# The order of work inside a tick of a fused convolution and wavelet kernel: the channel mix between two Toeplitz products, the group sums and signs at the tick's begin

## The chip, the cores and the metric

The kernel runs on one core of a Trainium2 chip. The metric is device time in microseconds (us); lower is better. Before the change three runs took 2979.06, 2980.12 and 2980.6 us, so the median is 2980.12 us. One further execution was profiled, and all rows of the profile come from it.

Engines are called as the profile calls them: PE is the matrix engine and PEld its weight loads, DVE is VectorE, ACT is ScalarE, SP is the queue that issues nearly all DMAs.

## The reference, cut to what matters

Four layers act on x, which has 4 batches, 64 channels and 256 by 256 pixels, all in float32. Layers 0, 1 and 3 are long convolutions. Their kernels are outer products of a row filter and a column filter, so each is two products with Toeplitz matrices, one along each axis, plus x times a bias per channel. Layer 2 goes to Haar coefficients, scales them, mixes the 64 channels, thresholds, and goes back:

```python
f1 = haar2d(x)
acc = jnp.zeros_like(f1[:, :conv_w.shape[1]])
for i in range(v.shape[0]):                              # 2
    f3 = f1 * v[i]
    f4 = jnp.einsum('bchw,oc->bohw', f3, conv_w[i])
    f5 = jnp.sign(f4) * jax.nn.relu(jnp.abs(f4) - tau[i])
    acc = acc + f5
y = haar2d(acc, inverse=True)
return y + x
```

Since v does not depend on the channel, the kernel applies it after the mix: "products with v" below are scalings of the mixed coefficients.

## The kernel before, in words

**Units.** The convolution stages work on one channel of one batch at a time. A channel goes through five stages, one tick apart: its loads; the first product of layer 0 (PSUM tile pa, copied by ACT at line 199 to the SBUF tile a0); the second product of layer 0 (PSUM tile py, read by DVE at line 212 to y0); the first product of layer 1 (pa again, copied to a1); the second product of layer 1 (py, read to y1) with the sums and differences of pairs (lines 257 and 258). Below, a0, y0, a1 and y1 name these tiles, and pa0, py0, pa1 and py1 their products on PE. Each product is four matmul calls (lines 190 and 191), eight instructions. Further stages follow a channel later: Haar levels on four channels at a time (lines 269 and 270), a split into two parts (ACT line 280, DVE line 281), a product pz (line 288), its copy (ACT line 296) and its store (line 297).

The mixing stage works on groups of four coefficient rows of one batch, 64 groups a batch. `mix` multiplies with the channel weights (PSUM tile px, line 340) and scales with v: four of sixteen columns by one DVE instruction (line 357), twelve by one ACT instruction each (line 359); for the last batch ten and six. `shrink` takes the magnitude and the sign on ACT (lines 365 and 366) and subtracts tau on DVE (line 367). `signed` multiplies both (line 372), and `add` sums the two terms into z (line 376). These four stages of a group are also one tick apart.

**Stages of the run.** First the convolutions of batch 0 alone. Then, for each batch b, the mixing of b runs together with the convolutions of batch b+1, and after it the inverse of b (lines 390 to 440) with what is left of them. In the mixing of batch 0 the 64 channels of batch 1 are spread over 82 ticks; in those of batches 1 and 2 the channels of the next batch are spread over 72 ticks, so that about one tick in nine starts no channel. With the last batch's mixing run 63 convolutions of layer 3 that were put off.

**Order.** Nothing is issued at once. Every stage of every unit is put on a list as (tick, place, number), and the list, sorted, gives the program order (line 497). Within a tick a lower place comes first. The convolution stages have the places 0 (loads), -1 (pa0), -2 (py0), -3 (pa1), -4 (py1). A scheduler then takes instructions of each engine by that priority as it believes their inputs and buffers to be ready, and adds the waits; what it makes of the list is fixed when the program is built, and each engine and DMA queue then works strictly through its own list. Tiles rotate through buffers: four PSUM buffers for pa, py and pz, two for px, two SBUF buffers for a0 and a1 together, five for the Toeplitz tiles, three for y0, two each for the tiles of magnitudes and of signs.

Of the kernel before, what the change touches and what calls it, by code (L numbers as in the profile page):

```python
# [37 lines left out]
def conv_seq_kernel(ctx, tc, x, fz, fw, bias, decay, haar, haar_row, factors, vt, taut, wmix, out):  # L38
# [189 lines left out]
    def at(tick, place, run, unit):  # L228
        events.append((tick, place, len(events), run, unit))
# [86 lines left out]
    def mixing(b, start, n_act):  # L316

        st = {}

        def load(g):  # L320
            f = mx.tile([P, 2, S], F32, name=f"f_{b}_{g}", tag="f", bufs=3)
            nc.sync.dma_start(f, coef[b].rearrange("k c p w -> (k c) p w")[:, 2 * g : 2 * g + 2])
            st[g] = {"f": f}
            if g % GT == 0:
                t = mx.tile([P, 2, GT, 16], F32, name=f"vt_{b}_{g}", tag="vt")
                nc.sync.dma_start(t, scales[g // GT])
                st["vt", g // GT] = t

        def scale(g, i):
            return st["vt", g // GT][:, i, g % GT, :]  # L330

        def over(g, i, n):
            return scale(g, i)[:, :n].unsqueeze(2).to_broadcast([P, n, C])

        def mix(g):
            f = st[g]["f"]
            ps = psx.tile([P, 2, 2, S], F32, name=f"px_{b}_{g}", tag="mix")
            for q in range(2):
                for h in range(2):
                    nc.tensor.matmul(  # L340
                        ps[:, h, q, :],
                        f[:, q, h * P : (h + 1) * P],
                        wb.rearrange("p r n -> p (r n)"),
                        start=True,
                        stop=True,
                    )
            if g == 0:

                one, two = ps[:, :, 0, :P], ps[:, :, 0, P:]
                d = mx.tile([P, 2, P], F32, name=f"d_{b}", tag="mag")  # L350
                nc.vector.tensor_copy(d, two)
                nc.vector.tensor_sub(two, one, d)
                nc.vector.tensor_add(one, one, d)
            f4 = mx.tile([P, 16, C], F32, name=f"f4_{b}_{g}", tag="f4")
            px = ps.rearrange("p h q (r i o) -> p (h q r i) o", r=2, i=2)
            n = 16 - n_act
            nc.vector.tensor_tensor(f4[:, :n], px[:, :n], over(g, 0, n), ALU.mult)  # L357
            for j in range(n, 16):
                nc.scalar.mul(f4[:, j], px[:, j], scale(g, 0)[:, j : j + 1])  # L359
            st[g]["f4"] = f4  # L360

        def shrink(g):
            f4 = st[g]["f4"]
            mag = mx.tile([P, 16, C], F32, name=f"mag_{b}_{g}", tag="mag")
            nc.scalar.activation(mag, f4, AF.Abs)  # L365
            nc.scalar.activation(f4, f4, AF.Sign)  # L366
            nc.vector.tensor_sub(mag, mag, over(g, 1, 16))  # L367
            st[g]["mag"] = mag

        def signed(g):  # L370
            mag = st[g]["mag"]
            nc.vector.scalar_tensor_tensor(mag, mag, 0.0, st[g]["f4"], ALU.max, ALU.mult)  # L372

        def add(g):
            parts = st.pop(g)["mag"].rearrange("p (h r i) o -> p h r i o", h=2, i=2)
            nc.vector.tensor_add(z[:, :, 4 * g : 4 * g + 4, :], parts[:, :, :, 0, :], parts[:, :, :, 1, :])  # L376

        for g in range(S // 4):
            at(start + g - 2, 0, load, g)
            for s, stage in enumerate([mix, shrink, signed, add]):  # L380
                at(start + g + s, -1 - s, stage, g)

    def inverse(b, start, put_off):

# [98 lines left out]
    start = ready + 3  # L483
    for b in range(B):
        mixing(b, start, 12 if b + 1 < B else 6)
        end = start + groups + 3
        if b + 1 < B:
            ready = convolutions(b + 1, spread(ahead, end + 2), in_parts=range(C), border=end)
        else:
            convolution(  # L490
                [(i, c) for i in range(B - 1) for c in sorted(put_off)], spread(start - 2, end + 2, (B - 1) * len(put_off))
            )
        inverse(b, end, put_off if b + 1 < B else ())

        start = max(end + C, ready + 3)
        ahead = start - 3
# [111 lines left out]
```

## Time and profile before

| | |
|---|---|
| median of three runs | 2980.12 us |
| profiled execution | 2980.9 us, of which span 2979.1 us |
| PE busy | 2919.6 us (98%) |
| DVE busy | 2546.2 us (85%) |
| ACT busy | 2168.8 us (73%) |
| DMA | 218 GB/s on average |
| mixing of batches 0, 1, 2, 3, first to last product with v | 459 to 862, 1096 to 1534, 1772 to 2211, 2445 to 2719 us |

A busy PE is not PE at its peak: matmuls overlap each other, and their ends are modelled, so that a short stop is partly hidden in the durations. The idle time of an engine is put down to the last thing it waited for. The three figures of a wait are the sum in us, the number of times, and the longest.

### The profile page before, as it was taken

The page shows a single profiled execution, that of the slowest core. Times are in us where ns is not written, and L with a number is a line of the kernel's source. Part 1 is how long each engine was busy: PE and PEld are TensorE (multiplying, and loading weights), DVE is VectorE, ACT ScalarE, POOL GpSimd, SP SyncE. Part 2 cuts the span into 40 slices and gives each one's busy share as a digit, 9 for nine tenths or more (in the row PEclk, how much of TensorE's full clock was granted, in tenths as well). Part 3 has the DMA queues.
Part 4 walks back from the last instruction along what each step waited for, and adds up shares of the span by engine and source line. Part 5 has one row for each costly group of instructions (what it writes and reads, how often), then busy time and mean ns, then how long its engine had stood idle before and what let it go on. Part 6 is the DMA issues. An engine that isn't in the chain of part 4 may idle for free. (4 is left out here: it accounts for less than half of the span.)

```text
span 2979.1 us, 51970 instructions
## 1 busy us (share of the span) xinstructions
PE 2919.6 (98%) x16950; PEld 2614.5 (88%) x16950; DVE 2546.2 (85%) x4571; ACT 2168.8 (73%) x5014; POOL 0.2 (0%) x4
## 2 busy tenths in 40 slices
PE   8999999999999999999999999999999999999999
PEld 6899988888888988888888988888888988888998
DVE  4767768999998879999989878999988889998776
ACT  2333338999986668999986758999986768887554
POOL 0000000000000000000000000000000000000000
PEclk9999999999999999999999999999999999999999
DMA  5877776666667876666667876666767877777766
GB/s 157 253 232 227 231 228 215 204 208 198 204 204 245 249 216 204 208 211 204 210 211 244 254 218 197 208 214 204 207 214 236 255 232 233 233 230 219 211 212 186
DMA packets 562497, 649.73 MB, mean 218 GB/s; under 512 B 44369, under 2 KB 447412, under 8 KB 562100
## 3 DMA queue, kind: packets, MB, share of 16 engines
q1 hardware_dynamic: 482996, 562.07, 63.6%
q10 hardware_dynamic: 79232, 84.34, 8.0%
q8 instruction: 137, 2.24, 0.3%
q14 instruction: 132, 1.08, 0.1%
HBM read 426.77 MB, written 219.48 MB: 217 GB/s over the span
## 5 line engine op out<-in xcount | busy, mean ns | idle before, releaser
L190 PE MATMUL py<-t,a 128*128 128x256 f32 x3072 | 928.4, 384 | 30.5 <-ACT a L199 26.1
L199 ACT COPY a<-pa 128x512 f32<-128x512 f32 x768 | 477.1, 623 | 411.6 <-PE pa L191 382.0
L359 ACT ACTIVATE f<-px,vt 128x64 f32<-128x64 f32 x2688 | 582.9, 353 | 108.5 <-DVE f L357 108.2
L191 PEld LDWEIGHTS py<-t,a 128*128 128x128 f32 x3072 | 583.3, 190 | 79.4
L191 PE MATMUL py<-t,a 128*128 128x128 f32 x3072 | 590.0, 274 | 0.0
L190 PEld LDWEIGHTS py<-t,a 128*128 128x128 f32 x3072 | 487.3, 191 | 85.6 <-ACT a L199 52.6
L340 PE MATMUL px<-wb,f 128*128 128x256 f32 x2048 | 496.5, 380 | 4.3 <-ACT f L359 4.3
L340 PEld LDWEIGHTS px<-wb,f 128*128 128x128 f32 x2048 | 365.0, 191 | 43.6 <-ACT f L359 6.8
L367 DVE TENSOR_TENSOR mag<-mag,vt 128x1024 f32<-128x1024 f32 x256 | 312.7, 1222 | 22.5 <-ACT mag L365 18.7
L403 ACT CAST w<-pw 128x512 fp32r<-128x512 f32 x256 | 150.4, 587 | 225.1 <-PE pw L401 218.9
L372 DVE SCALAR_TENSOR_TENSOR mag<-mag,f 128x1024 f32<-128x1024 f32 x256 | 312.0, 1219 | 1.1
L190 PE MATMUL pa<-t,y 128*128 128x256 f32 x1024 | 306.5, 381 | 2.0 <-DVE y L212 2.0
L190 PE MATMUL pa<-t,x 128*128 128x256 f32 x1024 | 305.5, 380 | 0.9 <-issue 0.9
L365 ACT ACTIVATE mag<-f 128x1024 f32<-128x1024 f32 x256 | 292.0, 1141 | 9.4 <-DVE z L376 6.8
L393 ACT COPY zc<-z 128x512 f32<-128x512 f32 x256 | 281.8, 1102 | 2.0 <-ACT w L403 1.2
L366 ACT ACTIVATE f<-f 128x1024 f32<-128x1024 f32 x256 | 275.3, 1075 | 5.8 <-DVE y L212 0.7
L281 DVE TENSOR_TENSOR sp<-sd,sp 128x512 fp32r<-128x512 f32 x256 | 176.3, 689 | 102.1 <-ACT sp L280 99.2
L190 PE MATMUL pa<-t,u 128*128 128x256 f32 x772 | 232.7, 383 | 3.2 <-PE pu L413 1.9
L212 DVE SCALAR_TENSOR_TENSOR y<-x,bsb,py 128x512 f32<-128x512 f32 x256 | 190.4, 744 | 44.9 <-PE py L191 37.9
L417 DVE SCALAR_TENSOR_TENSOR t<-r,pu 128x512 f32<-128x512 f32 x256 | 175.1, 684 | 59.7 <-PE pu L413 56.2
L212 DVE SCALAR_TENSOR_TENSOR y<-y,bsb,py 128x512 f32<-128x512 f32 x256 | 190.1, 743 | 33.1 <-PE py L191 32.3
L191 PEld LDWEIGHTS pa<-t,x 128*128 128x128 f32 x1024 | 194.6, 190 | 26.3
(67 smaller groups left out, 4470.2 us busy)
## 6 DMA issues: line engine op xcount, KB each, us to landing
t<-pad SPq DMA_DIRECT2D x768, 256.0 KB, 4.0
x<-in_x SPq DMA_DIRECT2D x256, 256.0 KB, 4.1
keep<-sd SPq DMA_DIRECT2D x256, 256.0 KB, 2.7
coef<-co SPq DMA_DIRECT2D x256, 256.0 KB, 3.2
f<-coef SPq DMA_DIRECT2D x256, 256.0 KB, 3.9
r<-keep SPq DMA_DIRECT2D x256, 256.0 KB, 3.3
out_y<-y ACTq DMA_DIRECT2D x256, 256.0 KB, 3.6
late<-u ACTq DMA_DIRECT2D x63, 256.0 KB, 2.7
```

Of the source, the lines that this page charges most:

```text
L190: nc.tensor.matmul(ps[:, m, :], src[:, 0, m * P : (m + 1) * P], t[:, ::-1], start=True, stop=False)
L191: nc.tensor.matmul(ps[:, m, P:], src[:, 1, m * P : (m + 1) * P], t[:, : P - 1 : -1], start=False, stop=True)
L199: nc.scalar.copy(a, ps)
L212: nc.vector.scalar_tensor_tensor(y, s[res], bsb[:, layer, c : c + 1], ps, ALU.mult, ALU.add)
L281: nc.vector.tensor_tensor(w[:, 1], t, w[:, 0].bitcast(F32), ALU.subtract)
L340: nc.tensor.matmul(ps[:, h, q, :], f[:, q, h * P : (h + 1) * P], wb.rearrange("p r n -> p (r n)"), start=True, stop=True,)
L359: nc.scalar.mul(f4[:, j], px[:, j], scale(g, 0)[:, j : j + 1])
L365: nc.scalar.activation(mag, f4, AF.Abs)
L366: nc.scalar.activation(f4, f4, AF.Sign)
L367: nc.vector.tensor_sub(mag, mag, over(g, 1, 16))
L372: nc.vector.scalar_tensor_tensor(mag, mag, 0.0, st[g]["f4"], ALU.max, ALU.mult)
L393: nc.scalar.copy(a, z[:, :, :, c].rearrange("p h (i k) -> p h k i", k=2))
```

## The change

The four stages of a group get other places within their ticks. The ticks themselves, the instructions, the tiles and the buffers stay.

```diff
         for g in range(S // 4):
             at(start + g - 2, 0, load, g)
-            for s, stage in enumerate([mix, shrink, signed, add]):
-                at(start + g + s, -1 - s, stage, g)
+            for s, (place, stage) in enumerate([(-2.5, mix), (-3.5, shrink), (-4.1, signed), (-4.2, add)]):
+                at(start + g + s, place, stage, g)
```

In program order a tick was: add, py1 and pair sums, signed, pa1, shrink, py0, mix, pa0, loads, levels, split and pz. It becomes: add, signed, py1 and pair sums, shrink, pa1, mix, py0, pa0, loads, levels, split and pz. So `mix` moves from behind py0 to between pa1 and py0, `shrink` ahead of pa1, and `signed` ahead of py1. ACT's products with v come from behind y0's place to between the copy of a1 and the copy of a0.

## The prediction

> **What bounds the kernel now.** I read the page first, then busy time by stage, the waits of each mixing stage, and the timeline where a wait ends.
>
> ```profile
> PE 2919.6 (98%) x16950; PEld 2614.5 (88%) x16950; DVE 2546.2 (85%) x4571; ACT 2168.8 (73%) x5014; POOL 0.2 (0%) x4
> ```
>
> PE is the bound, and nothing here changes its work, so only its stops can be won. Busy time in the mixing of batches 0 and 1:
>
> ```profile
> 459.00:862.00 403.00, 393.46 (x2158) 346.92 (x2157) 385.94 (x668) 379.72 (x1075) 0.00 (x0) 1.00 0.67 202
> 1096.00:1534.00 438.00, 433.70 (x2412) 387.68 (x2411) 407.86 (x714) 391.19 (x1094) 0.00 (x0) 1.00 0.68 207
> ```
>
> The columns after the length are PE, PEld, DVE and ACT. DVE (96% and 93%) and ACT (94% and 89%) are nearly as full as PE, so a late instruction there reaches PE. Which ones, says the list of waits of the first of these stages:
>
> ```profile
> PEld py L190 <- ACT a L199: 18.4, 29, 2.1
> ...
> PE py L190 <- ACT a L199: 9.2, 13, 1.7
> ...
> PEld pa L190 <- DVE y L212: 1.4, 4, 0.5
> ...
> PE pa L190 <- DVE y L212: 0.2, 1, 0.2
> ```
>
> A second product waits for ACT's copy of the first; a first product nearly never waits for DVE's y0. One such stop in the timeline:
>
> ```profile
> 514.61 0.42 DVE L357 TENSOR_TENSOR f<-px,vt 128x256 f32<-128x256 f32 x1
> ...
> 515.06 2.57 ACT L359 ACTIVATE f<-px,vt 128x64 f32<-128x64 f32 x12 [0.54 <-DVE f L357]
> ...
> 517.44 0.67 ACT L199 COPY a<-pa 128x512 f32<-128x512 f32 x1
> ...
> 518.16 0.70 PE L190 MATMUL py<-t,a 128*128 128x256 f32 x2 [0.83 <-ACT a L199]
> 518.70 0.38 PE L191 MATMUL py<-t,a 128*128 128x128 f32 x2
> ```
>
> pa0 was over at 514.2, but its copy stands behind twelve products with v (2.57 us), which had waited for DVE. py0 needed it three products later.
>
> **What the Trainium skill says.** "TensorE: Matmul & The Clock Gate", section "Architectural detail: the array is 16× 32×32, not 1× 128×128", says that ACT and DVE are strict FIFO, while PE can pull weight loads ahead. The copy at 517.44 agrees. "Perfetto Trace Analysis", section "Identifying the Most-Contended Engine", warns that PE's busy share is no measure of its headroom, since pipelined matmuls look smaller; so I price a stop from start to start. Neither page prices a reordering.
>
> **The change part by part.** No instruction is added or removed. The inverse stages and the convolutions of batch 0 keep their order in the built program; only the mixing stages change.
>
> *Step 1, what can be won.* PE's idle time before a second product that waited for a copy is 9.2 us in 13 stops (batch 0), 4.2 in 13 (batch 1), 5.9 in 15 (batch 2): 19.3 us in 41. At 518.16 the idle time is 0.83, but py0 starts 0.99 later than after an unhindered product, and its second half comes after 0.54 instead of 0.43: 1.10 in all, 0.27 more than shown. 19.3 + 41 x 0.27 = 30.4 us is the ceiling of this step.
>
> *Step 2, a0 gets time.* Below, a pace is the distance of two starts on an engine that waits for nothing; it is some 0.08 under the shown duration, since instructions overlap (1.14 for the 1.22 of L367). From the timeline of a full tick without a stop (1236.5 to 1243.9), start to start: px 1.73, pa0 1.22, pz 0.55, py1, pa1 and py0 1.31 each; together 7.43. Before, PE's cycle is px, pa0, pz, py1, pa1, py0: between the end of pa0 and py0 lie 0.55 + 1.31 + 1.31 = 3.17. After, it is px, py0, pa0, pz, py1, pa1, px, py0: 4.90. ACT's list stays products, copy a0, copy of pz, split, then magnitude, sign and copy a1. With px from 0, its result at 1.93 (results come 0.2 after the next product's start), DVE's part to 2.4, twelve products at a pace of 2.37 to 4.8, the copy ends at 5.3. Before, py0 starts at 6.12: 0.8 to spare, and DVE has only to be 0.8 late, as at 514.61 (about 1.6 late). After, py0 starts at 9.16: 3.9 to spare. The worst of the 41 copies was late by 1.7 beyond its 0.8, which is 2.5, still under 3.9: step 1 is won whole.
>
> *Step 3, a1 loses nothing.* Between pa1 and py1 lie py0, px, pa0 and pz before and after: 4.81. Where shrink now precedes its copy, magnitude and sign (0.97 pace each) delay it to 8.7 in this count; py1 starts at 12.24: 3.5 to spare.
>
> *Step 4, y0 pays.* Between py0 and pa1 lay px, pa0, pz, py1: 4.81. Now pa0, pz and py1: 3.08. Besides, in DVE's list y0 now stands behind L367, L357 and often L372, the multiplication with the sign, which waits for ACT. Paces: y1 0.66, split 0.61, sums 0.67, L367 1.14, L357 0.34, L372 1.13. From y1 at 6.33: split to 7.6, sums to 8.3, L367 (its magnitude is ready at 7.2) to 9.4, L357 to 9.75, L372 (sign ready at 8.2) to 10.9, y0 to 11.6. pa1 starts at 13.55: 1.9 to spare. Next on DVE come add 0.60 and about 1.0 of levels, to 13.2; y1 can begin at 13.76. A full tick costs nothing.
>
> *Step 5, the ticks around a missing channel.* Two px follow each other sooner, and ACT's 4.3 us for a group is not shortened. Laid out in the same way over nine ticks of batch 1 (px of two groups 6.2 instead of 7.4 apart, ACT at work on one group's signs while the next px is done), y0 ends 0.5, 0.2 and 0.5 us before pa1 needs it in three ticks, and more elsewhere. Each wait of one engine for another adds some 0.1 that I left out, so I take 0.2 us of new stops in nine ticks: 192 / 9 x 0.2 = 4 us. A stop before pa1 pushes everything behind it by the same amount, ACT and DVE catch up meanwhile, and it isn't paid twice. Bounds: 0, and as many stops as step 1 removes (30 us), if these spares are all overdrawn.
>
> *Step 6, the rest.* The Toeplitz tile for pa1 lands 4.0 us after its issue, and its buffer comes free 10 us ahead of use: nothing, and PE waited for no such DMA before. The level step waits for the store of its input: before, it starts 3.4 to 4.8 us after the sums, and after, by the count of step 4, about 3.3, against 2.7 from issue to landing and 0.4 to the issue. That is tight: it can hold DVE, with y1 and the split behind it, by some tenths in a part of the 48 level steps. DVE's spare of 0.6 in a tick (step 4) takes most of that; I allow 1 us. The moved stages issue no DMAs, and in SP's list the others shift by a place or two only. Every px has two ticks until its buffer is needed again, as before, and a0 and a1 find their shared buffers free, since on PE py0 still precedes the next pa0, and py1 the next pa1. In the mixing of batch 3 DVE is busy 267.83 of 274 us and its list keeps its order after the first 15 groups: 0, between -3 and +3.
>
> Sum: -30.4 + 4 + 1 = -25 us. On the profiled 2980.9 that is 2956; the median of the runs is 0.8 lower, so I write 2956 for both.
>
> **The rivals.**
>
> *DVE sets the pace (same).* If DVE and its own waits were the limit in these stages, PE would stop before pa1 for as long as it stopped before py0. For: 96% and 93% busy; at 514.61 it was DVE that was late. Against: PE hardly waited for DVE, and DVE's paces sum to 57.6 us in nine ticks with eight channels, 3.6 a channel (two y, sums, split, levels) and 3.2 a group (L367, L357, L372, add), against PE's 8 x 5.70 + 9 x 1.73 = 61.2. Time: 2980, give or take 6. That the change does not do what it says belongs here: the products stay ahead of a0's copy, and in some ticks a0 stood ahead of them before and now never does; if those ticks were the late ones, the 1.73 won in step 2 would be spent on 2.37 of products.
>
> *Half of it.* The spares of step 5 are overdrawn where ACT runs behind, mostly in batch 0, whose gaps come two in nine: 12 us of new stops, 2968.
>
> *y0 becomes the wait of every tick (slower).* y0 stands behind L372, that behind the sign on ACT, that behind the copies and twelve products. If this chain ran over 1.9 us later than laid out in full ticks, pa1 would stop in all of them. There are 49 + 57 + 57 = 163 y0 in the three stages; it decides from a mean stop of 30.4 / 163 = 0.19. At 0.3: +49 - 30, 2999. Against: in the tick of 514.61 DVE was 1.6 late, within the spare.
>
> **How the numbers follow.** About 6 us (0.2%) is what a measurement of this kernel can tell from no change. Forecast: 0.50 for 2946 to 2964. Half: 0.22, 2964 to 2974. Same: 0.15, 2974 to 2986. Slower: 0.10, around 2999. Better than 2946: 0.03, if the short stops of 0.1 after weight loads, which the ceiling leaves out, go too. Faster 0.75, same 0.15, slower 0.10. The range 2942 to 2984 leaves out the slower case, the tail of the better one and the edge of the same one. Since the shown signs differ, the forecast's own range is 2946 to 2964.
>
> **What would show it.** Step 2: in the waits of the mixing stages, PE's second product behind the copy falls from 9.2, 4.2 and 5.9 us to under 1 each. Step 4: first products behind y0 stay under 4 us in all; over 15 is the half case, over 30 the last rival. Step 6: the mixing of batch 3 keeps its 274 us within 3, and level steps wait for stores under 5 us in all. The mixing of batches 0, 1 and 2 shortens by about 11, 6 and 8 us. The prediction is wrong if PE's stops move to another wait, or if the copies stay late in spite of 1.73 us more.

## The result, and the profile after

The changed kernel takes 2974.56 us (median of 16 runs, 2971.16 to 2976.75) against 2980.05 us on the same chip: ratio 0.9978, 95% interval 0.9971 to 0.9985. That is 5.5 us less where 25 were predicted; it lies outside the forecast's 2946 to 2964 and inside the wider range of 2942 to 2984. The profiled span fell from 2979.1 to 2973.4 us. The page's first row of the changed kernel:

```profile
PE 2913.8 (98%) x16950; PEld 2615.1 (88%) x16950; DVE 2545.5 (86%) x4571; ACT 2156.9 (73%) x5014; POOL 0.2 (0%) x4
```

PE is as full as before and does the same work. Where its stops went is told by its groups (busy time, mean ns of one, idle time before them and what ended it):

```profile
L190 PE MATMUL py<-t,a 128*128 128x256 f32 x3072 | 919.0, 381 | 8.9 <-ACT a L199 5.5
...
L190 PE MATMUL pa<-t,y 128*128 128x256 f32 x1024 | 311.6, 386 | 22.4 <-DVE y L212 20.3
```

The same two rows of the kernel before:

```profile
L190 PE MATMUL py<-t,a 128*128 128x256 f32 x3072 | 928.4, 384 | 30.5 <-ACT a L199 26.1
...
L190 PE MATMUL pa<-t,y 128*128 128x256 f32 x1024 | 306.5, 381 | 2.0 <-DVE y L212 2.0
```

So most of the stop behind a0 is gone, and a stop behind y0 has come. In the list of waits of the mixing of batch 0 (459 to 862 us):

```profile
PEld pa L190 <- DVE y L212: 14.8, 20, 1.9
PE pa L190 <- DVE y L212: 8.1, 14, 1.5
PEld py L190 <- ACT a L199: 2.1, 6, 0.8
PE py L190 <- ACT a L199: 0.4, 1, 0.4
```

9.2 us behind a0 became 0.4, and 0.2 behind y0 became 8.1. In the mixings of batches 1 and 2 the stops behind a0 vanished, and 4.9 and 4.7 us behind y0 came. The busy time by stage, columns as before:

```profile
459.00:862.00 403.00, 393.56 (x2160) 348.11 (x2159) 386.57 (x667) 375.57 (x1074) 0.00 (x0) 1.00 0.68 203
1096.00:1534.00 438.00, 432.27 (x2415) 387.64 (x2414) 407.90 (x714) 387.80 (x1094) 0.00 (x0) 1.00 0.71 207
```

DVE holds the same 96% and 93%.

A busy row can't say how long a stage took, so I measured each stage in the records of PE, between the starts of the same matmuls in every kernel (for a mixing: from a product at its begin to the first product of the next inverse). Length in us:

| kernel | convolutions of batch 0 | mixing 0 | mixing 1 | mixing 2 | mixing 3 |
|---|---|---|---|---|---|
| before | 424.7 | 435.0 | 486.3 | 487.9 | 304.6 |
| after | 426.3 | 436.4 | 484.5 | 484.2 | 303.1 |
| change | +1.6 | +1.4 | -1.8 | -3.7 | -1.5 |

Predicted were -11, -6 and -8 for the mixings 0 to 2. The inverse stages agree within 1.2 us. Each length comes from one profiled execution. How far such a length scatters is told by the convolutions of batch 0: in the kernels before and after and in those of experiments 1 to 4 and 11 the engines do the same work there in the same order, and it took 424.7 to 427.5 us. So a difference of under 3 us in a single stage, the +1.6 and the +1.4 among them, says nothing.

One of the new stops, the longest of mixing 1, from its timeline (DVE's instructions, then PE's):

```profile
1200.72 0.37 DVE L269 TENSOR_TENSOR sd<-sd 128x128 f32<-128x128 f32 x1
1201.13 0.40 DVE L270 SCALAR_TENSOR_TENSOR sd<-sd 128x128 f32<-128x128 f32 x1
1201.56 0.28 DVE L269 TENSOR_TENSOR sd<-sd 128x64 f32<-128x64 f32 x1
1201.87 0.27 DVE L270 SCALAR_TENSOR_TENSOR sd<-sd 128x64 f32<-128x64 f32 x1
1202.18 0.22 DVE L269 TENSOR_TENSOR sd<-sd 128x32 f32<-128x32 f32 x1
1202.43 0.23 DVE L270 SCALAR_TENSOR_TENSOR sd<-sd 128x32 f32<-128x32 f32 x1
1202.56 0.69 DVE L281 TENSOR_TENSOR sp<-sd,sp 128x512 fp32r<-128x512 f32 x1
1203.16 0.75 DVE L212 SCALAR_TENSOR_TENSOR y<-y,bsb,py 128x512 f32<-128x512 f32 x1
1203.82 1.22 DVE L367 TENSOR_TENSOR mag<-mag,vt 128x1024 f32<-128x1024 f32 x1
...
1205.96 1.22 DVE L372 SCALAR_TENSOR_TENSOR mag<-mag,f 128x1024 f32<-128x1024 f32 x1
1207.09 0.75 DVE L212 SCALAR_TENSOR_TENSOR y<-x,bsb,py 128x512 f32<-128x512 f32 x1
```

```profile
1199.65 0.38 PE L191 MATMUL py<-t,a 128*128 128x128 f32 x2
...
1202.91 0.59 PE L190 MATMUL py<-t,a 128*128 128x256 f32 x2
...
1204.00 0.38 PE L191 MATMUL py<-t,a 128*128 128x128 f32 x2
1204.14 0.71 PE L288 MATMUL pz<-sp,hbr 128*128 128x512 f32 x2
1204.68 0.59 PE L190 MATMUL py<-t,a 128*128 128x256 f32 x2
...
1205.77 0.38 PE L191 MATMUL py<-t,a 128*128 128x128 f32 x2
1207.89 0.70 PE L190 MATMUL pa<-t,y 128*128 128x256 f32 x2 [1.74 <-DVE y L212]
```

This is a tick around a missing channel: between py0 (1202.91 to 1204.4) and pa1 PE has only pz and py1, no pa0. The product that y0 (at 1207.09) reads had ended by 1204.4, and PE could have begun pa1 at 1206.0; it began at 1207.89, 1.9 us late. DVE was behind already: y1 (1203.16) began 3.1 us after its product, of which the line at 1199.65 is the last part, had ended. Two things in DVE's list ahead of y0 stand out. L372, the multiplication with the sign, takes 1.13 from start to start. And the six level steps took 1.84 us (1200.72 to 1202.56): the last of them, with the split behind it, took 0.13, while the one before, of the same size but with a level step behind it that needs its result, took 0.25. Without such neighbours the six would have taken 1.22 by the paces given further below. 1.13 + 0.62 = 1.75 of the 1.9 us, worked out for this one stop.

So two theories stood against each other, besides the rival on record that DVE simply sets the pace. **P**: the place of L372 ahead of y0 costs the gain. **N**: level steps next to each other, each needing the one before, take longer than they were counted, and DVE is too full for it. The expectations below use letters of their own, and each says what it means by them. "The product with f4" in them is the multiplication with the sign, L372, and VectorE and ScalarE are DVE and ACT.

### The profile page after: what moved, and what is told of

It reads as the page before. It is cut to its first block, busy times and chain, and to the rows that moved or that the text cites. A ratio compares the mean times of both kernels' runs of the same rounds, so it can differ in the third digit from the quotient of the medians.

```text
span 2973.4 us, 52066 instructions
## 1 busy us (share of the span) xinstructions
PE 2913.8 (98%) x16950; PEld 2615.1 (88%) x16950; DVE 2545.5 (86%) x4571; ACT 2156.9 (73%) x5014; POOL 0.2 (0%) x4
## 5 line engine op out<-in xcount | busy, mean ns | idle before, releaser
L190 PE MATMUL py<-t,a 128*128 128x256 f32 x3072 | 919.0, 381 | 8.9 <-ACT a L199 5.5
L191 PEld LDWEIGHTS py<-t,a 128*128 128x128 f32 x3072 | 583.4, 190 | 79.3
L190 PEld LDWEIGHTS py<-t,a 128*128 128x128 f32 x3072 | 500.4, 191 | 50.9 <-ACT a L199 12.4
L340 PE MATMUL px<-wb,f 128*128 128x256 f32 x2048 | 488.2, 380 | 4.9 <-ACT f L359 4.9
L190 PE MATMUL pa<-t,y 128*128 128x256 f32 x1024 | 311.6, 386 | 22.4 <-DVE y L212 20.3
L372 DVE SCALAR_TENSOR_TENSOR mag<-mag,f 128x1024 f32<-128x1024 f32 x256 | 311.7, 1218 | 1.9
L366 ACT ACTIVATE f<-f 128x1024 f32<-128x1024 f32 x256 | 285.2, 1114 | 3.0
L281 DVE TENSOR_TENSOR sp<-sd,sp 128x512 fp32r<-128x512 f32 x256 | 176.1, 688 | 91.4 <-ACT sp L280 90.2
```

The source lines that it names most:

```text
L190: nc.tensor.matmul(ps[:, m, :], src[:, 0, m * P : (m + 1) * P], t[:, ::-1], start=True, stop=False)
L191: nc.tensor.matmul(ps[:, m, P:], src[:, 1, m * P : (m + 1) * P], t[:, : P - 1 : -1], start=False, stop=True)
L281: nc.vector.tensor_tensor(w[:, 1], t, w[:, 0].bitcast(F32), ALU.subtract)
L340: nc.tensor.matmul(ps[:, h, q, :], f[:, q, h * P : (h + 1) * P], wb.rearrange("p r n -> p (r n)"), start=True, stop=True,)
```

## The experiments

All ratios are to the kernel before, run on the same chip. The experiments ran on several chips, so kernels of different experiments are best compared by their ratios.

**1. The place of mix alone.**

```diff
-enumerate([(-2.5, mix), (-3.5, shrink), (-4.1, signed), (-4.2, add)])
+enumerate([(-2.5, mix), (-2, shrink), (-3, signed), (-4, add)])
```

> Only the mix is moved (place -2.5); shrink, signed and add keep the places of before. Theory A (the place of the mix does everything, and the stops before the second product became stops before pa1, behind y0): as the changed kernel, 2974 us within 3, PE's first products wait 15 to 22 us for y0 and its second products under 7 us for copies. Theory B (the sums and signs at the tick's begin fill DVE ahead of y0 and cause the new stops): 2955 to 2965 us, waits for y0 under 8 us.

Measured: 2972.96 us, ratio 0.9975 (0.9965 to 0.9985); 4.9 us behind a0, 18.8 behind y0. The place of `mix` does all that the change does, the gain and its loss, as theory A had it.

**2. The rest alone.**

```diff
-enumerate([(-2.5, mix), (-3.5, shrink), (-4.1, signed), (-4.2, add)])
+enumerate([(-1, mix), (-3.5, shrink), (-4.1, signed), (-4.2, add)])
```

> Shrink, signed and add are moved as in the change, the mix stays at -1. Theory A: as the kernel before, 2978 us within 3, PE's second products wait 18 to 28 us for copies, its first products under 5 us for y0. Theory B: slower than before, 2983 to 2992 us, since DVE is filled ahead of y1 and y0.

Measured: 2986.26 us, ratio 1.0019 (1.0012 to 1.0027), 6 us slower than before, where theory A expected no change. The list of waits of this kernel:

```profile
PE px L340 <- ACT f L359: 19.6, 22, 1.1
PE py L190 <- ACT a L199: 16.0, 28, 1.7
```

Stops behind a0 went down by 10 us, but px now waits for ACT's products with v (4.3 us before), probably because magnitude and sign stand ahead of them on ACT and px's buffer comes back late. This wait was in none of my theories; beside the moved `mix` it doesn't come (4.9 us in the kernel after).

**3. y0 ahead of the multiplication with the sign.** The kernel after, with L372 queued on DVE behind the newest y0; nothing else is held.

```diff
+    if new == "y0":
+        newest[0] = i.ins            # i: the instruction of line 212
...
-    nc.vector.scalar_tensor_tensor(mag, mag, 0.0, st[g]["f4"], ALU.max, ALU.mult)
+    with tc.issue_after(newest[0]):
+        nc.vector.scalar_tensor_tensor(mag, mag, 0.0, st[g]["f4"], ALU.max, ALU.mult)
```

> The changed kernel, with the multiplication by the sign (L372 of before) queued on DVE behind the newest y0; PE's order stays. Theory A1 (y0 is late because 1.1 us of a multiplication that nobody needs soon stands ahead of it): the stops of 0.4 to 0.7 us before pa1 vanish; waits of first products for y0 fall from 20.3 us to under 8; time 2952 to 2962 us. Theory A2 (DVE as a whole is too full around the level steps, so that any order makes something late): waits for y0 fall, but as much comes back as waits of second products, of px or of pz; time 2970 to 2978 us. Theory A3 (the level step's wait for the store of its input holds DVE): waits for y0 stay above 14 us; 2970 to 2975 us.

Measured: 2963.93 us, ratio 0.9945 (0.9932 to 0.9959). Its groups:

```profile
L191 PE MATMUL py<-t,a 128*128 128x256 f32 x3072 | 920.2, 381 | 10.2 <-ACT a L205 6.1
...
L191 PE MATMUL pa<-t,y 128*128 128x256 f32 x1024 | 310.7, 385 | 9.4 <-DVE y L218 8.5
```

Stops behind y0 fell from 20.3 to 8.5 us, and those behind a0 stayed away. In the timeline of mixing 1 y0 (L218) now stands ahead of the multiplication (L381):

```profile
1192.87 0.61 DVE L277 TENSOR_TENSOR sd<-sd 128x256 f32<-128x256 f32 x1
1193.40 0.74 DVE L218 SCALAR_TENSOR_TENSOR y<-x,bsb,py 128x512 f32<-128x512 f32 x1
1194.06 1.22 DVE L381 SCALAR_TENSOR_TENSOR mag<-mag,f 128x1024 f32<-128x1024 f32 x1
```

The mixings took 434.0, 480.0, 480.5 and 303.2 us: mixings 1 and 2 are 6.3 and 7.4 shorter than before, where the prediction had 6 and 8. Mixing 0 is 1.0 shorter, where it had 11.

**4. mix half and half.** Two of the four matmuls of px on each side of py0.

```diff
+    at(start + g, -2.5, lambda g: product(g, 0), g)      # q = 0
-    for s, (place, stage) in enumerate([(-2.5, mix), ...
+    for s, (place, stage) in enumerate([(-1.5, mix), ... # q = 1, and the scaling with v
```

> The changed kernel with the four matmul calls of the mix divided: two between pa1 and py0, two between py0 and pa0. The gap for a0's copy is then 4.0 us and the one for y0 3.9 us, instead of 4.9 and 3.1. Theory A (two gaps share one sum, and each engine's lateness decides): both kinds of stops are small, second products under 8 us, first products under 8 us; time 2955 to 2966 us. Theory A2 (total fullness decides): 2970 to 2978 us, stops divided between both.

Measured: 2978.37 us, ratio 0.9991 (0.9983 to 0.9999). Stops behind a0 14.0 us, behind y0 2.6, and 7.3 of second products that the list puts down to a level step. Stops behind y0 nearly vanish, but those of second products are 21 us again, and nothing is gained; neither expectation had that.

**5 and 6. Level steps left out**, of the kernel after and of the kernel before (the transform is then not complete).

```diff
-for s, steps in enumerate([(1,), (2, 4), (8, 16, 32, 64)]):
+for s, steps in enumerate([(1,), (2,), ()]):
```

> The kernel after, with the level steps 4 to 64 left out: a part of the transform is not computed, and ten of the fourteen level instructions of four channels go, some 2.8 us of VectorE for four channels or 5.7 us for nine ticks of mixing and convolution. Theory F (VectorE is nearly full: with 4.0 us a channel, the level steps one behind another included, nine ticks ask it for 60.8 of 61.2 us, so that every small delay reaches the next y0): the waits of first products for y0 fall from 20 us to under 6, and the time to about 2955. Theory Q (only the order counts: y0 stands behind the product with f4 in each full tick, however busy VectorE is): the waits for y0 stay at 15 to 22 us and the time lies within 4 us of 2974.

> The same left out of the kernel before (level steps 4 to 64 are not computed). Both theories: its stops for a0 have nothing to do with VectorE's load, so its time stays within 5 us of 2980. What counts is the difference of the two kernels without these steps, after less before: F -17 to -28 us (the gain that the prediction stated comes out when VectorE has room), Q -3 to -9 us as with them.

Measured: 2944.61 us, ratio 0.9877 (0.9862 to 0.9892), and 2954.73 us, ratio 0.9910 (0.9897 to 0.9924). Stops behind y0 fell to 6.0 us, as N has it. But the difference of the two is 10 us, between the expected bands, because the kernel before gained 27 us as well. I had said that its stops for a0 have nothing to do with DVE's load; its list of waits without these steps denies it (26.1 us with them):

```profile
PE py L190 <- ACT a L199: 8.7, 17, 1.5
```

A likely reason: a copy a0 is late on ACT where ACT's products with v, ahead of it, wait for DVE's product of the same group, as in the prediction's stop at 518.16; with DVE relieved, these waits of ACT fell from 108.2 to 88.6 us. In mixing 0 the two kernels then take 428.2 (before) and 428.4 us (after): no gain of the change shows there, with or without these steps. In mixings 1 and 2 it is worth 4.3 and 4.9 us.

**7 and 8. Level steps apart**, in the kernel after and in that of experiment 3. The steps go 4, 4, 4 and 2 instructions to a tick, each with its own place, and order edges put another DVE instruction between two of them where there is one; split and pz follow one tick later. Instructions are the same.

```diff
-for s, steps in enumerate([(1,), (2, 4), (8, 16, 32, 64)]):
-    at(after(end + 1 + s, n), 1, levels(steps), n)
+for s, steps in enumerate([(1, 2), (4, 8), (16, 32), (64,)]):
+    T = after(end + 1 + s, n)
+    slots = [(0, -2.2), (0, 1)] if s == 3 else [(0, 1), (1, -4.15), (1, -3.9), (1, -3.45)]
+    for i, (step, part) in enumerate((step, part) for step in steps for part in (0, 1)):
+        at(T + slots[i][0], slots[i][1], level(step, part), n)
```

> The kernel after with all its level steps, laid so that another VectorE instruction stands between two of them wherever one can be had (pairs of level steps next to each other fall from 384 to 196), each four channels in 4, 4, 4 and 2 instructions a tick instead of 2, 4 and 8, and the split and the half-band product one tick later. No instruction is added or taken away. F: each pair taken apart saves about 0.12 us, 23 us of VectorE over the program; two thirds of it lie in the mixings, the waits for y0 fall from 20 us to about 10 and the time from 2974.5 to about 2966. Q: waits and time as in the kernel after, within 3 us.

> The same level steps taken apart (367 pairs next to each other become 214) in the kernel of the third run, in which the product with f4 is queued behind the newest y0. F: the waits for y0 that were left there, 8.5 us, fall to about 4, above all in mixing 0, and the time from 2963.9 to about 2958. Q: within 2 us of 2963.9.

Measured: 2956.66 us, ratio 0.9919 (0.9905 to 0.9932), and 2958.59 us, ratio 0.9922 (0.9910 to 0.9935). The first was expected at 2966 and is the fastest complete kernel of this study, 25 us under the kernel before in the same runs. Its timeline shows level steps (L281 and L284) standing singly:

```profile
1201.86 0.18 DVE L284 SCALAR_TENSOR_TENSOR sd<-sd 128x16 f32<-128x16 f32 x1
1201.96 0.74 DVE L224 SCALAR_TENSOR_TENSOR y<-x,bsb,py 128x512 f32<-128x512 f32 x1
1202.62 0.17 DVE L281 TENSOR_TENSOR sd<-sd 128x8 f32<-128x8 f32 x1
1202.70 1.22 DVE L390 SCALAR_TENSOR_TENSOR mag<-mag,f 128x1024 f32<-128x1024 f32 x1
```

They cost 0.08 to 0.10 us from start to start. But these lines also show the flaw of the test: the new order has put y0 (1201.96) ahead of the multiplication (L390) as well, in 121 of 164 cases (59 in the kernel after), taking in the traces each multiplication with the y0 that the list has one tick earlier. (The expectation of experiment 12 counts otherwise and gives 88 of 158.) Nor is all of the gain N's: 6.8 of the 18 us against the kernel after fall in the convolutions of batch 0 (419.5 us), where nothing of the mixing runs. The first level step of a chain stands later in the new order and no longer holds DVE for a transfer there (26.6 us of idle before it in this stage of the kernel after, 1.0 here). But DVE's idle time before the split grew from 56.0 to 92.0 us, and in all it is only 4 us less; where the 6.8 us come from was not tested.

**9. The same ticks without taking apart.** 4, 4, 4 and 2 instructions to a tick, one behind another (398 neighbouring pairs; 384 in the kernel after, 196 in experiment 7).

```diff
-for s, steps in enumerate([(1,), (2, 4), (8, 16, 32, 64)]):
+for s, steps in enumerate([(1, 2), (4, 8), (16, 32), (64,)]):
```

> The kernel after with the level steps in 4, 4, 4 and 2 instructions a tick and the split and half-band product one tick later, as in the seventh run, but the steps of a tick one behind another: 398 pairs of level steps stand next to each other (384 in the kernel after, 196 in the seventh run). Theory N (neighbours: a level step that needs the one just before it takes 0.12 us more): the waits for y0 stay at 15 to 22 us, the time within 4 us of 2974.5. Theory B (bursts: eight level instructions in one tick hold up the next y0, four do not): waits for y0 under 8 us and about 2957 us, as in the seventh run. A time half way would say that each does a part.

Measured: 2975.12 us, ratio 0.9978 (0.9970 to 0.9985), 23.1 us behind y0. Smaller bursts and the later ticks of split and pz do nothing; it is the order that does.

**10. Level steps apart in the kernel before.** The edit of 7 on the other order of ticks.

> The kernel before with the level steps laid apart exactly as in the seventh run (327 neighbouring pairs become 238). It tells what the change itself is worth when VectorE has more room, without leaving anything out. If a0's stops in the kernel before are ScalarE's own, as the prediction had it, they stay at 20 us or more and the time falls by 8 us at most, in the first convolution, to 2972 or more; the change is then worth 15 us. If they too came from VectorE, through ScalarE's products with v that wait for VectorE's product of the same group, a0's stops fall to 8 to 12 us and the time to about 2962; the change is then worth 4 to 8 us, as without the relief.

Measured: 2980.08 us, ratio 0.9996 (0.9988 to 1.0005); the list of waits:

```profile
PE py L191 <- ACT a L211: 22.9, 42, 1.5
```

The convolutions of batch 0 are 5.6 us shorter, mixing 1 is 3.6 longer, and a0's stops stay. With the level steps laid apart the change is thus worth 0.9996 - 0.9919 = 0.0077, some 23 us. Experiment 6 and this one seem to disagree on what makes a0 late; they differ in size, which may be why. ACT's waits for DVE's products with v don't settle it: they fell to 93.8 us here, nearly as far as in experiment 6. Leaving ten of fourteen level instructions out gives DVE 5.7 us in nine ticks, taking 89 pairs apart gives the whole kernel 11 (an estimate, at 0.12 a pair).

**11 and 12. Both causes crossed.** The multiplication with the sign pinned ahead of y0 in every tick that has both (`signed` moved up into the tick of `shrink`, y0 queued behind it), with level steps as they are, and apart.

```diff
-for s, (place, stage) in enumerate([(-2.5, mix), (-3.5, shrink), (-4.1, signed), (-4.2, add)]):
+for s, place, stage in [(0, -2.5, mix), (1, -3.5, shrink), (1, -2.2, signed), (3, -4.2, add)]:
```

> The kernel after with the product with f4 held ahead of y0 in every full tick (152 to 159 times, not some 130), its level steps left as they are (396 neighbouring pairs). It is the counterpart of the third run, in which that product stood behind y0 (2964 us). Theory P (the product's place ahead of y0 costs the mixings 1 and 2 their gain): waits for y0 at 20 us or more, 2975 to 2982 us.

> The same with the level steps laid apart as in the seventh run (200 neighbouring pairs): in the seventh run the product with f4 had come to stand behind y0 in 88 of 158 ticks, which mixed the two causes; here it stands ahead of y0 in nearly all. If the neighbours are a cause of their own (theory N), mixings 1 and 2 fall to 481 us each as in the seventh run, and the time to about 2958. If it was the product's place alone (P), they stay at 484 or more each, and only the first convolution and mixing 0 gain, some 8 us: 2966 or more.

Measured: 2984.14 us, ratio 1.0010 (1.0002 to 1.0018), and 2976.93 us, ratio 0.9986 (0.9980 to 0.9993). The pin has a price of its own in mixing 3, which takes 311.9 us in both (303.1 in the kernel after). So only mixings 1 and 2 are compared, as sums of the two, in us:

| | neighbours as they are | apart |
|---|---|---|
| multiplication ahead of y0 | 971.7 (exp. 11) | 965.4 (exp. 12) |
| ahead in 84 of 114 cases; in 32 when apart | 968.7 (after) | 960.9 (exp. 7) |
| behind y0 | 960.5 (exp. 3) | 960.8 (exp. 8) |

The waits of PE behind y0 in mixing 1 (1080 to 1540 us) go with it, first experiment 11, then 12:

```profile
PE pa L191 <- DVE y L219: 5.9, 14, 1.3
```

```profile
PE pa L191 <- DVE y L225: 2.5, 7, 0.4
```

P alone is worth 971.7 - 960.5 = 11.2 us, N alone 971.7 - 965.4 = 6.3, and both together no more than P: when either has given y0 its time back, the other has nothing left to give. Experiment 12 came out half way between its two expectations (481 or 484 each; 482.8 and 482.6). In both comparisons the two mixings agree: 6.2 and 5.0 us for P, 3.4 and 2.9 for N. So the place of the multiplication is shown as a cause, and it is the larger one in this comparison. That laying the level steps apart helps in mixings 1 and 2 is shown too, with neighbouring pairs down from 75 to 3 in each. But that layout also moves level steps to other places in DVE's list, and no experiment separates this from the price of a neighbour. It doesn't help everywhere: mixing 0 took 434.1 us in experiment 11 and 437.3 in experiment 12.

## Why the prediction was wrong

**Step 1 (what can be won) and step 2 (a0 gets time): right, and the ceiling too low.** The stops behind a0 in the mixings 0, 1 and 2 fell from 9.2, 4.2 and 5.9 us to 0.4, 0 and 0. In start-to-start terms the stops of second products were about 16, 11 and 13 us before, some 40 in all (the ceiling of 30.4 had counted only those put down to a copy), and about 3 after.

**Step 3 (a1 loses nothing): right.** No wait for the second copy shows in mixings 1 and 2, and at most the 0.4 us above in mixing 0.

**Step 4 (a full tick costs nothing): right in its result.** Call a cycle of PE full when px, py0, pa0, py1 and pa1 follow one another in it, pz aside. In the three mixings of the kernel after, 101 of the 173 products pa1 end a full cycle. Two of these were late, by 0.5 us together (counted as all stops below, from start to start and over 0.015 us). The spare that step 4 put at 1.9 us was smaller: y0 ended a median of 1.5 us before pa1 began in the full cycles of mixings 1 and 2, and 0.9 in those of mixing 0.

**Step 5 (the ticks around a missing channel): the step that failed.** It put the new stops at 0.2 us in nine ticks, 4 us in all. Measured were some 33 from start to start, about 14, 9 and 9 in the mixings 0, 1 and 2, or 1.5 in nine ticks. Of the 51 late products pa1, 49 lie around a missing channel (a few of them at a stage's edge), where PE's cycle is shorter: without pa0 only pz and py1 stand between py0 and pa1, 1.86 us by the prediction's paces instead of 3.08. In mixings 1 and 2 nearly every missing channel brings two stops, the first of 0.4 to 1.9 us and one of 0.3 some 11 us later. So the place and the wait were foreseen, and the size was not. The bound written beside the 4, "as many stops as step 1 removes", was where it went.

What the multiplication with the sign does to y0 in these ticks is shown by experiment 3, which puts it behind y0: the stops around missing channels fell from 9.1 and 9.0 us in mixings 1 and 2 to 2.6 and 3.1, while those of second products grew from 0.3 to 2.2 in each. A DVE that is behind keeps L372 ahead of y0 all the same, for the list is fixed; in the stop shown above 1.13 us of the 1.9 were only to be had by putting it behind.

A second term was off, the levels of step 4. They were entered as "about 1.0" a tick, with one channel in a tick, which is their mean without neighbours. From the records of the kernel after, start to start where the next instruction waits for no other engine, medians in us:

| level instruction, elements a partition | 512 | 256 | 128 | 64 | 32 | 16 | 8 |
|---|---|---|---|---|---|---|---|
| another instruction behind it | 0.60 | 0.53 | 0.30 | 0.18 | 0.13 | 0.10 | 0.09 |
| a level step behind it, which needs it | 0.73 | 0.67 | 0.43 | 0.31 | 0.25 | 0.22 | 0.21 |

In mixings 1 and 2 of the kernel after 66 pairs in 14 chains are neighbours, so a chain takes some 4.5 us instead of 3.9. Nine ticks then ask DVE for about 57.6 + 2 x 0.6 = 58.8 of 61.2 us (an estimate from these paces). That is still room on the mean; it is short where a chain's small steps fall into a short cycle. The prediction does not print its layout of these nine ticks, so how much of the 29 us each term accounts for stays open.

**Step 6: right.** Mixing 3 is 1.5 us shorter (0, give or take 3), and in the mixings level steps waited for stores for 3.8 us (under 5). The test should have said that it means the mixings: over the whole kernel this wait was 21 us before and is 18 after, most of it in the convolutions of batch 0.

**The rivals.** "DVE sets the pace" was argued away with a sum of paces 57.6 against 61.2. In mixing 0 experiments 5 and 6 fit it: both orders gain 7 to 8 us from a relieved DVE and end alike. But even there no full cycle made pa1 wait. In mixings 1 and 2 it doesn't hold: experiment 3 takes nothing from DVE and brings the gain predicted there. "Half of it" named the right wait and the right ticks, but put it at 12 us and mostly in batch 0. The time of 2974.6 lies between the two. By stages, the 20 us that are missing are 12 in mixing 0 and 4 each in 1 and 2; for these 8 experiment 3 shows the cause.

**What stays open** is mixing 0. Neither the place of the multiplication (434.0) nor level steps apart (431.2) bring its 11 us, and without small level steps no gain of the change shows there (428.2 and 428.4). With y0 ahead of the multiplication 10.7 us of its stops around missing channels were left. Which of DVE's many small delays hold it was not tried further.

The Trainium skill, "Perfetto Trace Analysis", section "Identifying the Most-Contended Engine", had been used to price PE's stops from start to start; the stage lengths above bear that out, since PE's busy share stayed at 98% in every complete kernel from 2957 to 2986 us.

## What to carry to other kernels

When a reordering buys one operand time, it takes it from the next one in the cycle: lay out that operand's whole queue, ask which instruction ahead of it nobody waits for soon (here the multiplication with the sign), and move that one behind it. Lay out the irregular ticks with the same care as the full one: where a unit is missing, the cycle of the engine that waits is shorter, and here nearly all of the new stops lay there. A spare worked out for an engine that begins on time is no spare on one that is 93% to 96% busy. And count chains of small instructions that need one another at their pace as neighbours.

## What the runs showed of the hardware

In these traces a level step that needs the result of the DVE instruction just ahead of it starts 0.12 to 0.14 us later than an instruction that doesn't, whatever the size of the one ahead; from start to start it is 0.73 against 0.60 us for 512 elements a partition, 0.21 against 0.09 for 8. The Trainium skill, "Perfetto Trace Analysis", section "Optimizing Scalar/DVE Operations", says that a profiled duration is longer than the engine's busy time, since the acknowledgement of the write overlaps with the next instruction. The traces agree for an independent one (0.60 from start to start for 0.69 shown); a dependent one gets no overlap and starts 0.03 after the shown end (0.73). The 93 sums that stand right behind the y1 they read start 0.03 after its end too. For the smallest level steps the dependence more than doubles the price, and the shown durations don't tell it: level steps of 32 elements have a mean of 217 ns in the kernel after, where 90 of 128 have such a neighbour, and 216 in experiment 7, where 26 have. It can be read from starts alone.
